# A four-stage attention and mixture-of-experts kernel: other queues and order for the first loads, a search by four experts, and another layout of the experts' weights

## The chip, the cores and the metric

The kernel runs on one core of a Trainium2 chip, as one launch. The metric is the device time of that core in microseconds (us); lower is better. A core has TensorE (PE; its weight loads are listed apart as PEld), VectorE (DVE), ScalarE (ACT), GpSimd (POOL) and SyncE (SP), which work side by side and wait for each other by semaphores. DMA transfers are issued by an instruction of SP, ACT or POOL and then run on 16 shared DMA engines.

## The reference

There are 8192 tokens (16 sequences of 512) with 256 features each, all in fp32. Four layers follow each other, each with a layernorm in front and a residual sum behind it:

```python
x = x + attention(layernorm(x))          # 16 heads of 16, rotary embedding, softmax
x = x + moe(layernorm(x))                # 64 experts
x = x + forget_attention(layernorm(x))   # linear attention with forget gates
x = x + moe(layernorm(x))                # the same weights as the second layer
```

The mixture of experts (`moe`) is the part that most of the change touches:

```python
probs = softmax(x @ router_w.T)                      # (T, 64)
topk_w, topk_ids = top_k(probs, 8); topk_w /= topk_w.sum(-1)
# each expert takes its first C = 128 tokens, in the order of the tokens
g, u = xb @ w_gate[e], xb @ w_up[e]                  # 256 -> 192
y = (silu(g) * u) @ w_down[e]                        # 192 -> 256
out = segment_sum(y * topk_w) + shared(x)            # shared: one expert for all tokens
```

The order of the 192 hidden features of an expert does not matter to the result, as long as gate, up and down agree on it.

## The kernel before, in words

`main` (L1453 to L1471) runs four stages one after the other. In the fast memory, data lies on 128 partitions.

**Stage 1, `attention` (L144 to L462).** The tokens are taken in 16 blocks of 512, and a block in 16 steps. Two tables, `dense` (L388) and `routed` (L403), say which piece of work stands at which step: `(queries, 1, 2)` at step 2 means chunk 2 of the projection of the block after this one. The loop runs them under `tc.manual_schedule`, which keeps the written order for the engines that it names (PE, DVE and ACT); for SP and POOL a scheduler puts the instructions in order. For each chunk of 128 tokens, `queries` projects (L229), copies (L237) and applies the rotary embedding with four operations on POOL (L242, L250 twice, L258) into a `pad`, which PE transposes (L283). Six pads are set to zero at the start (L179). The first loads are issued by SP: `wqkv_sb` (L168), `wo_sb` (L170), `rope_sb` (L172), x (L208), and ahead of them in the program the 32 small loads of `forget_bias` (L475), a bias of stage 3. mT, the row of maxima, is stored into the row qT by SP in each step group.

**`Part` (L1182 to L1426)** holds the router's and the shared expert's work for a routed stage: `moments`, `normed`, `features`, `logits` (L1313), `likely` (the softmax, L1325 to L1338), `choose` (top 8), `count`, `added` (running counts), `shared` (L1391) and `down` (L1413). In stage 1 it is woven into the attention's steps by the table `routed`. Its constructor loads the router's and the shared expert's weights by ACT's queue, and stores zeros behind the tokens (L1237). `Part.slots` (L1255) makes room for pairs of experts' weights; `Part.fetch` (L1266) loads a pair in three pieces by SP: gate, up and down, 384 KB each.

**Stage 2, `routed` (L873 to L1148).** The rest of the router's work for the last block comes first. The counts of tokens per expert and chunk of 128 tokens are stored and read back as `cw` (64 chunks on the partitions): L920 for all blocks but the last, L1130 for the last. `find` (L933 to L986) then searches the tokens of eight experts (`many = 8`): DVE compares `cw` (L942 to L947), PE picks the chunk's counts by matmuls (L954, L961), DVE counts and adds (L971 to L985), in two halves of four experts. `place` runs pieces of `find` between other work. The experts' loop has three steps in flight: `gather` (POOL, indirect load of 128 token rows, L998), `turned` (PE transposes, L1009), `widened` (gate and up, L1022: eight fp32 matmuls, each of two passes with a weight load of its own), `narrowed` (down, L1038, and an indirect scatter-add by POOL, L1049). The stationary operand of L1022 is the weights:

```python
lhsT=wm[:, e % 2, kd, ts(m % 2, FP)],     # FP = 96 of the FF = 192 columns, side by side
of = self.w_down[es].rearrange("e (k p) f -> p e k f", p=FP)
```

Pairs of weights ahead of the loop: 7 in stage 2, 4 in stage 4.

**Stage 3, `forget_attention` (L482 to L855)**, and **stage 4**, `routed` with `loads=True`: it loads x from stage 3's output (L914), does the router's work in 16 blocks, reads the counts back (L920), and runs the same experts' loop. `joined` (L1152) adds the two results and stores the output.

Of the kernel before, what the change touches and what calls it, by code (L numbers as in the profile page):

```python
# [9 lines left out]
F32 = mybir.dt.float32  # L10
# [27 lines left out]
class Block:  # L38


    def __init__(self, ctx: ExitStack, tc: tile.TileContext, T: int):
# [20 lines left out]
        self.stats = ctx.enter_context(tc.tile_pool(name="stats", bufs=2))  # L62
# [81 lines left out]
    def attention(self, x, x1, wqkv, wo, rope, part):  # L144
# [10 lines left out]
        with ExitStack() as c:  # L155
# [12 lines left out]
            nc.sync.dma_start(out=wqkv_sb, in_=wqkv.rearrange("(k p) f -> p k f", p=P))  # L168
            wo_sb = w.tile([P, KD, D], F32, name="wo_sb")
            nc.sync.dma_start(out=wo_sb, in_=wo.rearrange("(k p) f -> p k f", p=P))  # L170
            rope_sb = f1.tile([P, CB, 2 * HD], F32, name="rope_sb")
            nc.sync.dma_start(out=rope_sb, in_=rope.rearrange("(c p) f -> p c f", p=P))  # L172
# [4 lines left out]
            for i in range(CB + 2):  # L177
                pad = f1.tile([P, 2 * H, HP], F32, name=f"pad{i}")
                nc.gpsimd.memset(pad, 0.0)  # L179
                nc.gpsimd.memset(pad[:, H : 2 * H, HD : HD + 1], 1.0)  # L180
                pads.append(pad)
# [44 lines left out]
            def queries(b, i):  # L226
# [13 lines left out]
                t1 = f1.tile([P, 2 * H, HD], F32, name="t1")  # L240
                t2 = f1.tile([P, 2 * H, HD], F32, name="t2")
                nc.gpsimd.tensor_tensor(  # L242
# [5 lines left out]
                for half in range(2):  # L248
                    lo = half * (HD // 2)
                    nc.gpsimd.tensor_tensor(  # L250
                        t2[:, :, lo : lo + HD // 2],
                        qk2[:, :, :, 1 - half],
                        rope_sb[:, i, HD + lo : HD + lo + HD // 2]
                        .unsqueeze(1)
                        .to_broadcast([P, 2 * H, HD // 2]),
                        ALU.mult,
                    )
                nc.gpsimd.tensor_tensor(pads[b % 2][i][:, :, 0:HD], t1, t2, ALU.add)  # L258
# [104 lines left out]
            def output(b, i):  # L363
# [27 lines left out]
                3: [(queries, 1, 3)],  # L391
# [12 lines left out]
                0: [(part.added, -3), (part.likely, -2)],  # L404
                1: [(part.shared, -2, 0)],
                3: [(part.shared, -2, 1)],
# [6 lines left out]
                15: [(part.logits, -1)],  # L413
# [19 lines left out]
            with tc.manual_schedule(  # L433
                engines={nc.tensor.engine, nc.vector.engine, nc.scalar.engine}
            ):
                weights = (part.fetch(n, i) for n in range(3) for i in range(3))
                for s in range(-2 * steps, self.nblk * steps):
                    for count, n, work, *args in each(s):
                        if 0 <= n < count:
                            work(n, *args)  # L440
# [10 lines left out]
                part.likely(z - 1)  # L451
# [12 lines left out]
    def forget_bias(self, bqk):  # L464

        nc = self.nc
        sb = self.const.tile([P, 6], F32, name="bqk_sb")
# [11 lines left out]
        return sb  # L479
# [393 lines left out]
    def routed(self, part, loads=False):  # L873
# [7 lines left out]
        iota_c, down1, pairs = part.iota_c, part.down1, part.pairs  # L881
        with ExitStack() as c:

            def pool(n, **kw):
                return c.enter_context(
                    tc.tile_pool(name=f"f_{n}", bufs=n, side="left", **kw)
                )

            part.slots(pairs - len(part.slot), "left")
            w = c.enter_context(tc.tile_pool(name="f_w", bufs=1, side="left"))  # L890
# [3 lines left out]

            far = 4.0 * T
            first = w.tile([nch, 1], F32, name="first")
            nc.vector.tensor_scalar(first, self.iota_p[0:nch], float(P), far, ALU.mult, ALU.add)

            spare = w.tile([P, 1], F32, name="spare")
            nc.vector.tensor_scalar(spare, self.iota_p, far + T - P, None, ALU.add)  # L900
# [24 lines left out]
            many = 8  # L925
# [7 lines left out]
            def find(e0):  # L933
# [14 lines left out]
                yield  # L948
                cnt = self.small.tile([P, many], F32, name="cnt")
                place = self.small.tile([P, many], F32, name="place")  # L950
                for k0 in range(0, many, 4):
                    pn, ph = bank(), bank()
                    for k in range(k0, k0 + 4):
                        nc.tensor.matmul(  # L954
                            pn[:, ts(k - k0, P)],
                            lhsT=lies[:, k, :],
                            rhs=cw[:, e0 + k, :],
                            start=True,
                            stop=True,
                        )  # L960
                        nc.tensor.matmul(  # L961
                            ph[:, k - k0 : k - k0 + 1],
                            lhsT=lies[:, k, :],
                            rhs=first,
                            start=True,
                            stop=True,
                        )
                    yield
                    ks = slice(k0, k0 + 4)
                    near = p1.tile([P, 4, P], F32, name="near")  # L970
                    nc.vector.tensor_scalar(  # L971
                        near,
                        pn.rearrange("p (k t) -> p k t", t=P),
                        self.iota_p,
                        None,
                        ALU.is_le,
                    )
                    nc.vector.tensor_reduce(cnt[:, ks], near, AX.X, ALU.add)
                    nc.vector.scalar_tensor_tensor(
                        place[:, ks], ph[:, 0:4], -far, cnt[:, ks], ALU.add, ALU.add  # L980
                    )
                    yield
# [32 lines left out]
            def widened(e):  # L1015
# [3 lines left out]
                for m in range(4):  # L1019
                    wm = (wg, wu)[m // 2]  # L1020
                    for kd in range(KD):
                        nc.tensor.matmul(  # L1022
                            gu[:, m, :],
                            lhsT=wm[:, e % 2, kd, ts(m % 2, FP)],
# [36 lines left out]
            with tc.manual_schedule(  # L1061
# [4 lines left out]
                    nc.gpsimd.engine,  # L1066
                }
# [28 lines left out]
                if loads:  # L1096
                    for b in range(-4, nb + 1 + lag):
# [10 lines left out]
                        if nb - 4 <= b < nb:  # L1108
                            fetch(b - nb + 4)
                        if b == nb:  # L1110
                            chunks_before()
                            place(0, many)
                else:
                    z = nb - 1
                    for n in range(3, 5):
# [11 lines left out]
                    for i in range(CB):  # L1127
                        at = z * CB + i
                        queue = (nc.scalar, nc.sync)[i % 2]
                        queue.dma_start(out=cw[at : at + 1], in_=part.cum[:, ts(i, P)])  # L1130
                    part.shared(z, 1)
                    for n in range(5, pairs):
# [3 lines left out]
                    part.down(z, 0)  # L1136
                    place(0, many)
                    part.down(z, 2)
                ahead = 6
                for e in range(-ahead, E):  # L1140
                    run(e + ahead, E, gather)
                    place((e + 14) // many * many, 1)
# [39 lines left out]
class Part:  # L1182
# [6 lines left out]
    def __init__(self, ctx, k, x, y, weights, room, pairs, side):  # L1189
# [3 lines left out]
        nc, tc, T = k.nc, k.tc, k.T  # L1193
        self.pools = {
            n: ctx.enter_context(tc.tile_pool(name=f"r_{n}", bufs=n, side=side))
            for n in sorted({1, *room.values()})
        }
        w = self.pools[1]
        self.rows = k.dram.tile([T + P, ROW], F32, name="rows")
        self.counts = k.dram.tile([E, k.nch, P], F32, name="counts")  # L1200
        self.rw_sb = w.tile([P, KD, E], F32, name="rw_sb")
        nc.scalar.dma_start(out=self.rw_sb, in_=rw.rearrange("(k p) f -> p k f", p=P))

        self.wsg_sb = w.tile([P, KD, 2 * FF], F32, name="wsg_sb")
        for to, of, n in ((0, 0, FF), (FF, FF + P, FT), (2 * P, FF, P)):
            nc.scalar.dma_start(
                out=self.wsg_sb[:, :, to : to + n],
                in_=ws_gu[:, of : of + n].rearrange("(k p) f -> p k f", p=P),
            )
        self.wsd_sb = w.tile([P, 2, D], F32, name="wsd_sb")  # L1210
        nc.scalar.dma_start(out=self.wsd_sb[:, 0, :], in_=ws_down[0:P, :])
        nc.gpsimd.memset(self.wsd_sb[FT:P, 1, :], 0.0)
        nc.scalar.dma_start(out=self.wsd_sb[0:FT, 1, :], in_=ws_down[P:FF, :])

        self.hidden = []
        for i in range(room["hT"]):
            hT = w.tile([P, 2, BLK], F32, name=f"hT{i}")
            nc.gpsimd.memset(hT[FT:P, 1, :], 0.0)
            self.hidden.append(hT)
        self.iota_c = w.tile([k.nch, CAP], F32, name="iota_c")  # L1220
        nc.gpsimd.iota(
            self.iota_c,
            [[1, CAP]],
            base=0,
            channel_multiplier=0,
            allow_small_or_imprecise_dtypes=True,
        )

        self.down1 = w.tile([k.nch, k.nch], F32, name="down1")
        nc.gpsimd.memset(self.down1, 0.0)  # L1230
        nc.gpsimd.tensor_copy(self.down1[:, 1:], k.ident[0 : k.nch, 0 : k.nch - 1])

        with tc.tile_pool(name="r_z", bufs=1, side=side) as pz:
            zeros = pz.tile([P, ROW], F32, name="zeros")
            nc.gpsimd.memset(zeros, 0.0)
            for z in (self.rows, x, y):
                nc.scalar.dma_start(out=z[T : T + P, :], in_=zeros[:, 0 : z.shape[1]])  # L1237
# [14 lines left out]
        self.bank = None  # L1252

# [12 lines left out]
    def fetch(self, n, piece):  # L1266
# [6 lines left out]
        else:  # L1273
            to = both[0:FP, 2 * size :].rearrange("p (e k f) -> p e k f", e=2, k=2)
            of = self.w_down[es].rearrange("e (k p) f -> p e k f", p=FP)
# [154 lines left out]
def hybrid_block_kernel(  # L1430
# [29 lines left out]
    bqk_sb = k.forget_bias(b_bqk)  # L1460
    with ExitStack() as c:
        part = Part(c, k, attended, routed, moe, ROOM, 7, "right")
        k.attention(x, attended, a_wqkv, a_wo, rope, part)
# [79 lines left out]
```

## Time and profile before

| | us |
|---|---|
| median of 3 runs | 2860.42 (2859.69 to 2862.93) |
| profiled execution | 2867.78 |
| its span | 2865.9 |
| PE busy | 2595.7 |
| PEld busy | 1615.1 |
| DVE busy | 1870.4 |
| ACT busy | 1167.5 |
| POOL busy | 896.5 |
| TensorE clock granted, mean | 0.945 |

The page shows one execution, and everything read from it is compared with that execution's own 2867.78. Stage 1 ends near 1425 us, the experts' loop of stage 2 near 1720, stage 3 near 2270, the loop of stage 4 near 2790, and the rest is the final sum. Lines of a group read: engine, line, operation, output and inputs, shape, count. In the lines of the timeline the first number is the start, the second the time that the group takes, and the brackets hold the engine's idle time before it and what ended that.

### The profile page before, as it was taken

To read this page: it belongs to the slowest core of one execution; us is meant where nothing else is said; L and a number is where in the kernel's file an instruction comes from. 1 tells how busy PE (TensorE), PEld (TensorE's weight loads), DVE (VectorE), ACT (ScalarE), POOL (GpSimd) and SP (SyncE) were. 2 spreads that over 40 slices of the span, in tenths; PEclk is the share of its full clock that TensorE was granted. 3 is DMA by queue.
4 is the path that set the end of the run, shared out by engine and by line. 5 is a ranking of instruction groups with operands and counts; after the bars stand their busy time and mean duration, and the time that the engine had idled before them with its cause. 6 is when DMAs were issued, how large, how long until landed. Compare 5 with 4: busy or idle time off the path is not lost. (4 is left out here: it accounts for less than half of the span.)

```text
span 2865.9 us, 49079 instructions
## 1 busy us (share of the span) xinstructions
PE 2595.7 (91%) x18756; PEld 1615.1 (56%) x18756; DVE 1870.4 (65%) x4546; ACT 1167.5 (41%) x2291; POOL 896.5 (31%) x870
## 2 busy tenths in 40 slices
PE   4999999999999999999979986999999688879970
PEld 2444545544445544445459973666676565569860
DVE  2666666766666666666445636999999577845531
ACT  1565555655555655555512222334333212212220
POOL 4222221222221212220027775223322011127763
PEclk8899999999999999998979998999999879989995
DMA  1000111100111100001269973011110355339978
GB/s 60 1 6 21 33 34 35 32 20 20 34 33 34 33 20 27 27 25 35 68 164 255 257 168 105 25 48 54 48 38 20 96 164 134 99 100 255 253 176 344
DMA packets 210873, 243.75 MB, mean 85 GB/s; under 512 B 32847, under 2 KB 200911, under 8 KB 207567
## 3 DMA queue, kind: packets, MB, share of 16 engines
q1 hardware_dynamic: 181263, 192.22, 22.5%
q0 software_dynamic: 24576, 37.77, 6.7%
q10 hardware_dynamic: 4800, 10.62, 1.0%
q8 instruction: 150, 2.46, 0.4%
q14 instruction: 84, 0.69, 0.1%
HBM read 155.15 MB, written 84.74 MB: 84 GB/s over the span
## 5 line engine op out<-in xcount | busy, mean ns | idle before, releaser
L308 DVE TENSOR_REDUCE mx<-sc 128x1 f32<-128x512 f32 x1024 | 635.4, 682 | 418.0 <-PE sc L294 417.4
L334 ACT ACTIVATE pT<-sc 128x512 f32<-128x512 f32 x1024 | 528.7, 604 | 208.6 <-PE sc L294 206.8
L294 PE MATMUL sc<-kT,qT 16*128 16x512 f32 x2048 | 329.6, 607 | 1.7 <-DVE mx L308 1.7
L294 PE MATMUL sc<-qT,kT 17*128 17x512 f32 x2048 | 313.2, 647 | 0.0
L80 POOL TENSOR_SCALAR va<-mv 128x4 f32<-128x4 f32 x64 | 14.5, 226 | 765.2 <-DVE mv L74 540.1
L1022 PE MATMUL pb<-xeT,ws 128*96 128x128 f32 x2048 | 248.5, 275 | 0.2 <-DVE xeT L1011 0.2
L344 PE MATMUL sc<-pT,v 128*32 128x512 f32 x2048 | 239.6, 609 | 0.0
L1022 PEld LDWEIGHTS pb<-xeT,ws 128*96 128x96 f32 x2048 | 235.5, 166 | 0.6 <-DVE xeT L1011 0.4
L294 PEld LDWEIGHTS sc<-kT,qT 16*128 16x128 f32 x2048 | 159.5, 188 | 112.8 <-issue 62.3
L731 DVE SCALAR_TENSOR_TENSOR pT<-sc,of,left 128x256 f32<-128x256 f32 x512 | 205.8, 472 | 9.4 <-PE sc L714 9.3
L242 POOL TENSOR_TENSOR t<-qk,rope_sb 128x512 f32<-128x512 f32 x64 | 81.0, 1266 | 400.0 <-ACT qk L237 398.5
L868 ACT ACTIVATE th<-pb 96x256 f32<-96x256 f32 (+2 forms) x162 | 67.6, 425 | 304.1 <-PE pb L1022 216.0
L690 PE MATMUL pb<-feat,wqk_sb 128*128 128x512 f32 x384 | 176.3, 594 | 2.6 <-DVE left L673 2.6
L869 DVE SCALAR_TENSOR_TENSOR th<-th,pb 96x256 f32<-96x256 f32 (+2 forms) x162 | 76.4, 472 | 153.0 <-ACT th L868 102.6
L998 POOL DMA_INDIRECT xe<-rows,token x128 | 137.0, 1071 | 101.1 <-DVE token L985 62.7
L344 PEld LDWEIGHTS sc<-pT,v 128*32 128x32 f32 x2048 | 61.0, 112 | 170.5 <-issue 121.2
L294 PEld LDWEIGHTS sc<-qT,kT 17*128 17x128 f32 x2048 | 91.5, 185 | 93.9 <-issue 48.1
L1356 POOL TENSOR_TENSOR wt<-pr,chosen 128x256 f32<-128x256 f32 x32 | 23.2, 724 | 356.1 <-DVE chosen L1351 356.1
L229 PE MATMUL sc<-wqkv_sb,feat 128*128 128x512 f32 x256 | 129.5, 631 | 4.9 <-DMA wqkv_sb<-in_a_wqkv 4.9
L1038 PE MATMUL pb<-ws,he 96*128 96x256 f32 x512 | 131.9, 379 | 1.2 <-DVE he L870 1.2
L698 ACT ACTIVATE ez<-pb,bqk_sb 128x512 f32<-128x512 f32 x96 | 66.0, 687 | 134.3 <-PE pb L690 134.3
L72 DVE BATCH_NORM_STATS2 bn<-x 128x6 f32<-128x256 f32 x256 | 89.0, 408 | 41.6 <-POOL x L599 23.3
(175 smaller groups left out, 4557.0 us busy)
## 6 DMA issues: line engine op xcount, KB each, us to landing
ws<-in_w_gate SPq DMA_DIRECT2D x64, 384.0 KB
ws<-in_w_up SPq DMA_DIRECT2D x64, 384.0 KB
ws<-in_w_down SPq DMA_DIRECT2D x64, 384.0 KB
rows<-xn SPq DMA_DIRECT2D x32, 512.0 KB
routed<-y SPq DMA_DIRECT2D x32, 512.0 KB
x<-in_x SPq DMA_DIRECT2D x16, 512.0 KB
attended<-x SPq DMA_DIRECT2D x16, 512.0 KB
x<-attended SPq DMA_DIRECT2D x64, 128.0 KB
```

What stands on the lines that cost most here:

```text
L72: nc.vector.bn_stats(st[:, c, :], xt[:, c, :])
L229: nc.tensor.matmul(pq, lhsT=xnTs[b][:, kd, ts(i, P)], rhs=wqkv_sb[:, kd, 0 : 2 * D], start=(kd == 0), stop=(kd == KD - 1),)
L242: nc.gpsimd.tensor_tensor(t1, qk, rope_sb[:, i, 0:HD].unsqueeze(1).to_broadcast([P, 2 * H, HD]), ALU.mult,)
L294: nc.tensor.matmul(scs[j], lhsT=lhs[at : at + high, ts(i, P)], rhs=rhs[at : at + high, :], start=True, stop=True,)
L308: nc.vector.tensor_reduce(mxs[n][:, j, i : i + 1], sc, AX.X, ALU.max, negate=True)
L334: nc.scalar.activation(pT[:, j, :], sc, AF.Exp, scale=float(HD) ** -0.5)
L344: nc.tensor.matmul(pav[ts(j, HP), :], lhsT=vs[b % 2][:, i, 4 * hg + j, :], rhs=pT[:, j, :], start=(i == 0), stop=(i == CB - 1),)
L690: nc.tensor.matmul(pq, lhsT=wqk_sb[:, kd, ts(m, P)], rhs=xnTs[b][:, kd, :], start=(kd == 0), stop=(kd == KD - 1),)
L731: nc.vector.scalar_tensor_tensor(pTs[n][:, :, ts(s8, HD)], sc[:, :, ts(s8, HD)], of[:, s8 : s8 + 1], here, ALU.mult, ALU.mult,)
L998: nc.gpsimd.indirect_dma_start(out=xes[e], out_offset=None, in_=rows, in_offset=bass.IndirectOffsetOnAxis(ap=token[:, e : e + 1], axis=0),)
L1022: nc.tensor.matmul(gu[:, m, :], lhsT=wm[:, e % 2, kd, ts(m % 2, FP)], rhs=xeT[:, kd, :], start=(kd == 0), stop=(kd == KD - 1),)
L1038: nc.tensor.matmul(py[:, 0:D], lhsT=he[:, m, :], rhs=wd[:, e % 2, m, :], start=(m == 0), stop=(m == 1),)
```

## The change

- The constants of the search (`iota_c`, `down1`, `first`, `spare`) and the tile of zeros are made once for both routed stages, by DVE in part.
- First loads: wqkv, rope and wo go to ACT's queue, in this order. The memsets of the pads go from POOL to DVE. The rotary embedding of block 0's chunks 1 and 3 goes to DVE, with a later tile as its scratch.
- `forget_bias` becomes a generator; two of its loads are issued per step once the first block is under way. The loads of the router's and the shared expert's weights and the stores of zeros become `Part.begin`, issued by SP one step into the second pipeline block (stage 1), or at the head of stage 4.
- `likely` follows `logits` at step 15; `shared(-2, 1)` is put ahead of `queries(1, 3)` at step 3.
- SP is named in `manual_schedule` in stages 1, 2 and 4, so its DMAs keep the program's order.
- `find` searches four experts, in five pieces instead of seven. Stage 2's loop starts with one search of four instead of one of eight, and so does stage 4's.
- The last block's counts are read into `cw` by ACT's queue alone.
- 13 pairs of weights ahead in stage 2 (8 in one place, 5 more in the room that `Part` frees), 11 in stage 4.
- w_down is read so that a partition gets hidden features 2p and 2p + 1, in one piece of 2 KB instead of two of 1 KB; the columns of gate and up are then taken with a stride of 2.

The core of the diff:

```diff
@@ attention
-            nc.sync.dma_start(out=wqkv_sb, in_=wqkv.rearrange("(k p) f -> p k f", p=P))
+            nc.scalar.dma_start(out=wqkv_sb, in_=wqkv.rearrange("(k p) f -> p k f", p=P))
...
-                nc.gpsimd.memset(pad, 0.0)
+                nc.vector.memset(pad, 0.0)
...
+                if b == 0 and i % 2:
+                    eng, both = nc.vector, p2.tile([P, CB, D], F32, name="tok")
...
+                else:
+                    eng = nc.gpsimd
...
-                3: [(queries, 1, 3)],
+                3: [(part.shared, -2, 1), (queries, 1, 3)],
...
-                0: [(part.added, -3), (part.likely, -2)],
+                0: [(part.added, -3)],
...
-                15: [(part.logits, -1)],
+                15: [(part.logits, -1), (part.likely, -1)],
...
+                    nc.sync.engine,
...
+                    if s == 1 - steps:
+                        part.begin()
+                    if s >= 0:
+                        next(later, None)
@@ routed
-            many = 8
+            many = 4
...
-                            lhsT=wm[:, e % 2, kd, ts(m % 2, FP)],
+                            lhsT=wm[:, e % 2, kd, m % 2 : FF : 2],
...
-                        if nb - 4 <= b < nb:
-                            fetch(b - nb + 4)
+                        if nb - 5 <= b < nb:
+                            fetch(b - nb + 5)
                         if b == nb:
                             chunks_before()
-                            place(0, many)
+                            place(0, 5)
...
-                        queue = (nc.scalar, nc.sync)[i % 2]
-                        queue.dma_start(out=cw[at : at + 1], in_=part.cum[:, ts(i, P)])
+                        nc.scalar.dma_start(out=cw[at : at + 1], in_=part.cum[:, ts(i, P)])
...
                     place(0, 4)
-                    part.down(z, 0)
-                    place(0, many)
-                    part.down(z, 2)
+                    down(z)
+                    place(0, 1)
+                part.own.close()
+                n = len(part.slot)
+                part.slots(pairs - n, "left")
+                for n in range(n, pairs):
+                    fetch(n)
...
-                    place((e + 14) // many * many, 1)
+                    place((e + 10) // many * many, 2)
@@ Part.fetch
-            of = self.w_down[es].rearrange("e (k p) f -> p e k f", p=FP)
+            of = self.w_down[es].rearrange("e (p k) f -> p e k f", k=2)
@@ main
-        part = Part(c, k, attended, routed, moe, ROOM, 7, "right")
+        part = Part(c, k, attended, routed, moe, ROOM, 13, "left")
...
-        part = Part(c, k, forgot, routed, moe, ROOMY, 4, "right")
+        part = Part(c, k, forgot, routed, moe, ROOMY, 11, "left")
```

## The prediction

> **What bounds the kernel now.** I read the page's head first, then the time by engine in slices, TensorE's waits, and the stretches in which TensorE is idle.
>
> ```profile
> span 2865.9 us, 49079 instructions
> PE 2595.7 (91%) x18756; PEld 1615.1 (56%) x18756; DVE 1870.4 (65%) x4546; ACT 1167.5 (41%) x2291; POOL 896.5 (31%) x870
> PE   4999999999999999999979986999999688879970
> ```
>
> TensorE works 91% of the span; the low slices are the start, the passages between stages (slices 20, 24, 31 to 32, 35) and the final sum, which has no TensorE work. The waits name what ended each pause (total, times, longest):
>
> ```profile
> PE pb L586 <- DVE tok L98: 30.8, 1, 30.8
> PE sc L199 <- DVE tok L98: 21.7, 1, 21.7
> PE pb L1304 <- DVE xn L98: 20.4, 3, 18.4
> PE pb L930 <- DMA routed<-y: 13.2, 1, 13.2
> PE pb L930 <- DMA cw<-cum: 12.4, 1, 12.4
> PE sc L283 <- POOL pad L258: 10.7, 3, 3.7
> PE sc L229 <- DMA wqkv_sb<-in_a_wqkv: 4.9, 1, 4.9
> ```
>
> No wait names the experts' weights: they arrive ahead of their use already. Two windows (length, then busy time of PE, PEld, DVE, ACT, POOL; clock; DMA share; GB/s), one inside attention and one in the experts' loop, show that TensorE is the bound in both:
>
> ```profile
> 60.00:1280.00 1220.00, 1218.26 (x7897) 600.92 (x7898) 821.13 (x1800) 706.29 (x1387) 284.02 (x317) 0.99 0.08 26
> 1500.00:1560.00 60.00, 58.89 (x456) 55.55 (x455) 36.88 (x79) 15.35 (x36) 45.92 (x33) 1.00 0.98 250
> ```
>
> So the change can gain only in the passages, and lose wherever it makes TensorE's own stream longer. PE's instructions are as many before and after (10,469 in both orders). The profiled execution took 2867.8 us (span 2865.9 and 1.9 around it), 7.4 above the median of 2860.4. I sum differences and take them off the median.
>
> **1. Start.** Three lines of the timeline (start, length, idle before):
>
> ```profile
> 6.57 17.43 SPq L475 DMA_DIRECT2D bqk_sb<-in_b_bqk  x32
> 28.86 9.07 PE L229 MATMUL sc<-wqkv_sb,feat 128*128 128x512 f32 x16 [4.91 <-DMA wqkv_sb<-in_a_wqkv]
> 13.35 1.84 POOL L179 MEMSET pad<- 128x1024 f32 x2 [6.74 <-DMA routed<-zeros]
> ```
>
> SP issues 32 small bias loads for 17.4 us ahead of wqkv, so the first projection starts at 28.86. Besides, the pads' memsets hold POOL to 19, because they wait for the zeros' store, and the layernorm's power (L80, L82) stands behind them. After: wqkv leaves first on ACT's queue, the biases follow two per step, and the memsets are DVE's. x then sets the start. It landed at 6.0; sharing the transfer engines with wqkv's 0.79 MB, I put it at 7. From there by before's rows: statistics 1.8, POOL 1.3, DVE 0.6, first tok 0.4 and 0.5 of hand-over, transposes and copies 2.9, so the projection begins at about 14.5 to 15.5: 13.5 gained. The six memsets that DVE takes on (POOL took 0.95 each) are 4 to 6 us, done by about 7, beside the load of x; if x landed earlier they would be next to wait for.
> Then rope: POOL turns the four chunks in series, 1.27 + 1.43 + 1.27 = 4.0 each with a hand-over, so the pads are ready 20.7 after the projection's start (49.56 less 28.86). With every second chunk on DVE (0.68 + 2 x 0.42 + 0.68 = 2.2 by its rows of those sizes) POOL has two: 3.8 + 0.6 + 8.1 = 12.6. Gain 8. Begin's nine transfers (rw to zeros) go to SP behind the first two x, at about 0.45 each, 4 us, ahead of the first qT<-mT, which isn't ready for 20 us yet. Start together: 21.5; I take 21, and 15 to 23.
>
> **2. Attention.** Its PE order differs by the place of one part.shared call. `likely` moves 1 step earlier in DVE's order (L1325 to L1338 are 1.5 us of DVE a block); DVE is busy 821 of 1220, so I cost it at nothing. If that cover were gone it would be 16 blocks x 1.5 = 24. SP now keeps program order, so a store that waits holds the next qT<-mT and x; x is asked for two blocks (152 us) ahead. 0, bound 0 to +5.
>
> **3. Into the first experts.**
>
> ```profile
> 1445.18 8.98 SPq L1422 DMA_DIRECT2D routed<-y  x1
> 1451.77 1.17 ACTq L1130 DMA_DIRECT2D cw<-cum  x2
> 1457.20 1.23 SPq L1130 DMA_DIRECT2D cw<-cum  x2
> 1463.68 1.22 DVE L942 TENSOR_TENSOR lies<-cw,iota_c 64x1024 f32<-64x1024 f32 x1 [8.66 <-DMA cw<-cum]
> ```
>
> SP sits 9 us in the store of y, so half of cw's last pieces are issued 5.4 late. All four on ACT end at 1451.8 + 4 x 0.6 = 1454.1 instead of 1458.4: 4.3 gained (ACT's silu behind them is 1.2 later; its hT waits 15 us for use). Search: tokens of eight experts take 16.5 us (1463.7 to 1480.2), with down(z) between its halves. For four: three half-size compares (1.22 to about 0.65 each), 3.4 of matmuls, 2.0 of DVE, about 7.9: 8.6 earlier. The next four move into the loop, where each expert's search is 8 matmul passes of 0.11 less overlap, 0.73 us: +2.9. Net 10. But the extra pairs (5 x 1.18 MB, some 23 us at 250 GB/s) now travel beside the first gathers, which land 4 to 8 us after issue; I leave 2 for that. Taken 8, bounds 3 and 11.
>
> **4. The loops: pairs ahead and 2 KB pieces.** The window shows DMA at 0.98, yet PE idles 1.1 of 60 us, so I cost both at nothing; the cover is the weights' existing lead. Were it gone (gathers late), row "L1009 <- DMA xe" holds only 10.5 us in all.
>
> **5. The loops: gate and up read at stride 2.** This is the dangerous edit, since these loads are TensorE's:
>
> ```profile
> 1542.33 1.80 PEld L1022 LDWEIGHTS pb<-xeT,ws 128*96 128x96 f32 x16
> 1545.37 0.30 PEld L961 LDWEIGHTS pb<-first,lies 64*128 64x128 f32 x2
> 1545.59 0.30 PEld L954 LDWEIGHTS pb<-cw,lies 64*128 64x128 f32 x2
> 106.32 0.20 PEld L128 LDWEIGHTS sc<-ident,oT 128*128 128x128 f32 x2 [0.76 <-ACT pT L334]
> 1547.02 0.32 PEld L1009 LDWEIGHTS pb<-ident,xe 128*128 128x128 f32 x2
> ```
>
> Read the spacing, not the length. L1022's 16 loads follow each other every 0.11 us, which is what their matmuls take. L954 and L961, half of whose matmuls have one column, show what a plain load needs when nothing else limits it: 0.11 for 128 columns, so by proportion 0.083 for 96; a load has 0.026 of slack. L1009 is the only load here at stride 2 (xe as "(p k)"). Two of them last 0.32, one 0.195 to 0.22, so the second starts about 0.10 after the first; the same transposing load without stride (L128: two in 0.20, one 0.14) has 0.06. Stride 2 costs about 0.04 per 128 columns there, or a factor 1.7. [...] But a strided transposing load at 0.10 is still no slower than a plain unstrided one at 0.11. [...] If the 0.04 adds (0.03 for 96 columns): 0.113 against 0.11, at most +0.06 an expert. If it multiplies: 0.083 x 1.7 = 0.14, +0.03 x 16 = +0.48 an expert. With the search in the loop PE's period is 3.55 and POOL's 3.16 (gather 0.98, scatter 1.58, 0.3 after each), later PE 2.85 against POOL's 3.16: 55 x 0.48 and 9 x 0.17 are 28 a stage, 56 in both. I take +1, because the nearest row of its own, the spacing at L1009, stays under the matmul's pace; both ends stay.
>
> **6. The other passages.** Forget attention starts when the last scatter has landed; after, its weights load and its POOL copies need not stand beside it, but x and y still wait: -2 (-4 to 0). Second routed stage: first x<-forgot is issued at 2275.92 behind three weight loads (1.2 MB) and lands 7.3 later; now behind nine smaller ones: -2 (-5 to 0). Its end: TensorE waits 13.2 for y and counts, then hides the first gathers under 27 us of shared work; shared starts some 4 earlier, four experts' search moves into the loop (+2.9): -1 (-4 to +4). The final sum (324 GB/s) is untouched.
>
> **Sum.** -21 + 0 - 8 + 0 + 1 - 2 - 2 - 1 = -33: profiled 2834.8, median 2827.4; I say 2828. The granted clock can move it: TensorE is at half clock in several stretches of 5 to 50 us after pauses (clock 0.63 in 2260 to 2300, 0.66 in 1440 to 1500), and when each ends is not set by the kernel; +-14.
>
> **The rivals.**
> (a) Slower: the strided load is TensorE's bound in both expert loops, from the point where a load needs over 0.11 us. Price +56 against my +1, so 2828 + 55 = 2883. For it: TensorE is the bound there (58.9 of 60) and the L1009 spacing grew 1.7-fold. Against: that spacing stays below a plain load's. Chance 0.20.
> (b) Only part of the start comes: x lands late behind wqkv, or the memsets hold DVE's statistics, and first gathers are slowed by the prefetch. Gain 10 to 15, about 2848. For it: both x and wqkv then share the transfer engines. Against: before, x landed at 6.0 with wo and the shared weights in flight. Chance 0.13.
> (c) The gains are eaten: SP in program order holds qT<-mT or x in each attention block by 2 us, 32 in all, near 2860. Against: TensorE idles 1.7 of 1220 us with stores on the same queue. Chance 0.07, of which half ends within 0.2%.
> (d) The change doesn't do what it says: more pairs ahead and longer pieces bring nothing, as no wait names weights. That is in my sum already; start and search remain. A gain over 50 would need the loops to have waited for DMA after all. Chance 0.02.
> The main case has 0.58, and its own range is 2812 to 2844.
>
> **The numbers.** About 0.2% (5.7 us) is what a measurement of this kernel tells from no change. Faster: 0.58 + 0.13 + 0.02 = 0.73. Same: 0.04. Slower: 0.20 + 0.03 = 0.23. Range: from 2808 (main case with the lucky clock) to 2884, which takes in the middle of (a); about 0.12 lies above, 0.05 below.
>
> **What would show it.** Right: the first L229 matmul (of after, L254) near 15 and the first use of the last pad near 28; token of the first experts about 13 us sooner after attention's last sum; L1022's successor still 16 loads in 1.80 us, and the window in the loop at 3.5 us an expert. Wrong: 16 loads in 2.2 us or more; PE waits on wqkv or qT; a wait of L1009's transposes for xe over 20 us in all.

## The result, and the profile after

The changed kernel takes 2885.5 us (median of 4 runs, 2882.6 to 2888.4) against 2860.6 (2859.7 to 2862.9): 24.9 us slower, ratio 1.0086, 95% interval 1.0068 to 1.0103. The forecast was 2828. The time lies 1.5 us above the range, close to rival (a)'s 2883, but rival (a)'s mechanism is not the one that made it.

The head of the page of the changed kernel, its profiled execution (2888.4, span 2886.2):

```profile
span 2886.2 us, 49094 instructions
PE 2597.3 (90%) x18756; PEld 1638.5 (57%) x18756; DVE 1896.4 (66%) x4641; ACT 1168.1 (40%) x2291; POOL 879.0 (30%) x849
PE   7999999999999999999689959999999688599980
```

The first slice went from 4 to 7, so the start was gained. PE's busy time is the same within 2 us, but only in the sum: between attention's first and last score matmul it is 22 us less (1336.6 against 1358.7), in the two experts' loops 31 more (453.9 against 422.7). TensorE's waits in the changed kernel (line of the waiting instruction, what it waited for, total, times, longest):

```profile
PE pb L987 <- DVE lies L983: 42.7, 30, 4.0
PE pb L628 <- DVE tok L122: 30.1, 1, 30.1
PE pb L966 <- DMA cw<-counts: 24.9, 1, 24.9
PE pb L966 <- DMA cw<-cum: 17.8, 1, 17.8
PE sc L224 <- DVE tok L122: 13.5, 1, 13.5
PE pb L1042 <- DMA xe<-rows,token: 1.7, 2, 1.2
```

L987 is the search's matmul (L954 before). Before, it waited

```profile
PE pb L954 <- DVE lies L947: 8.5, 3, 3.3
```

and none of the three lay inside a loop. Of the 30 now, 4 lie ahead of the loops; the other 26, 13 in each loop, are 1.2 us each, 31 us together. L966 (L930 before) waits longer in both routed stages: 24.9 where it was 13.2, and 17.8 where it was 12.4.

The same moments in both traces (us from the span's start), read from the timelines, say where the difference arose:

| moment | before | after | after less before | gained or lost on the way |
|---|---|---|---|---|
| first score matmul | 55.5 | 37.2 | -18.3 | -18.3 |
| last score matmul of attention | 1416.0 | 1375.3 | -40.7 | -22.4 |
| stage 2: first gate/up matmul | 1492.0 | 1450.2 | -41.8 | -1.1 |
| stage 2: last down matmul | 1709.9 | 1696.0 | -13.9 | +27.9 |
| stage 4: first router matmul | 2289.8 | 2273.3 | -16.5 | -2.6 |
| stage 4: counts of earlier chunks (L930, L966) | 2525.0 | 2520.0 | -5.0 | +11.5 |
| stage 4: first gate/up matmul | 2562.4 | 2559.4 | -3.0 | +2.0 |
| stage 4: last down matmul | 2782.2 | 2803.4 | +21.2 | +24.2 |
| end | 2865.9 | 2886.2 | +20.3 | -0.9 |

(The spans differ by 20.3, the medians by 24.9: the profiled execution of before lies 7 us above its median, that of after 3.) Up to the first experts the change is 42 us ahead, 13 more than forecast. The two loops give back 52, and the end of stage 4's router work 11.5. That attention is shorter is not luck with the clock: between its first and last score matmul the granted clock stands at half speed for 58.0 us in both traces.

The loop's windows, two of the changed kernel (length, busy PE, PEld, DVE, ACT, POOL, clock, DMA share, GB/s), against 58.89 of 60 and a clock of 1.00 before:

```profile
1500.00:1560.00 60.00, 55.15 (x397) 51.81 (x395) 33.57 (x79) 13.68 (x32) 42.05 (x33) 0.94 0.90 230
1560.00:1620.00 60.00, 56.41 (x399) 53.57 (x398) 31.16 (x75) 12.83 (x30) 38.85 (x31) 0.91 0.77 188
```

TensorE stands still for 4 to 5 us of 60, and its granted clock falls below 1. Its weight loads take no longer than before. The same stretch of the trace:

```profile
1520.90 1.78 PEld L1055 LDWEIGHTS pb<-xeT,ws 128*96 128x96 f32 x16
```

Sixteen loads at stride 2 take 1.78 us, where sixteen without stride took 1.80; the run with plain loads, below, settles it. One search, in order of time:

```profile
1523.83 1.91 PE L1055 MATMUL pb<-xeT,ws 128*96 128x128 f32 x16
...
1525.57 1.03 PE L1071 MATMUL pb<-ws,he 96*128 96x256 f32 x4
1526.19 0.42 DVE L911 SCALAR_TENSOR_TENSOR th<-th,pb 96x256 f32<-96x256 f32 x1 [0.44 <-ACT th L910]
1526.64 0.42 DVE L912 SCALAR_TENSOR_TENSOR he<-th,pb 96x256 f32<-96x256 f32 x1
1526.98 0.68 DVE L983 TENSOR_TENSOR lies<-lies,begun 64x512 f32<-64x512 f32 x1
1527.80 0.46 PE L987 MATMUL pb<-cw,lies 64*128 64x128 f32 x2 [1.20 <-DVE lies L983]
1527.81 1.59 POOL L1082 DMA_INDIRECT routed<-ye,token  x1 [2.13 <-DVE lies L983]
```

Read it backwards. PE waits 1.20 us for `lies`. DVE makes `lies` 0.68 us long, but only behind the two silu pieces of the expert whose gate and up matmuls PE finished just before, and those come behind ACT's part. So PE waits out a round trip through ACT and DVE that normally lies beside its next matmuls. The cause is in the call `place(..., 2)`: it issues two pieces of the search at once, and the second pair is the product on DVE and the matmuls on PE that need it. Before, one piece was issued per expert, and the product was one expert old when PE came to it:

```profile
1534.99 1.21 DVE L947 TENSOR_TENSOR lies<-lies,begun 64x1024 f32<-64x1024 f32 x1
1537.39 0.49 PE L954 MATMUL pb<-cw,lies 64*128 64x128 f32 x2
```

In the changed kernel POOL's scatter also stands 2.13 us, and the trace names `lies` for it too, so the delay isn't made up on its side.

### The profile page after: what moved, and what is told of

The parts are those of the page before. It is cut to its first block, busy times and chain, and to the rows that moved or that the text cites. A ratio compares the mean times of both kernels' runs of the same rounds, so it can differ in the third digit from the quotient of the medians.

```text
span 2886.2 us, 49094 instructions
## 1 busy us (share of the span) xinstructions
PE 2597.3 (90%) x18756; PEld 1638.5 (57%) x18756; DVE 1896.4 (66%) x4641; ACT 1168.1 (40%) x2291; POOL 879.0 (30%) x849
## 5 line engine op out<-in xcount | busy, mean ns | idle before, releaser
L328 PE MATMUL sc<-kT,qT 16*128 16x512 f32 x2048 | 307.8, 607 | 1.4 <-DVE mx L342 1.4
L1055 PE MATMUL pb<-xeT,ws 128*96 128x128 f32 x2048 | 273.4, 292 | 1.6 <-DVE xeT L1044 1.4
L1055 PEld LDWEIGHTS pb<-xeT,ws 128*96 128x96 f32 x2048 | 258.4, 182 | 4.0 <-DVE xeT L1044 1.7
L1031 POOL DMA_INDIRECT xe<-rows,token x128 | 130.9, 1023 | 125.9 <-DVE token L1018 88.1
L1082 POOL DMA_INDIRECT routed<-ye,token x64 | 102.7, 1605 | 74.7 <-ACT ye L1079 47.0
```

The lines of the kernel that those rows point to most:

```text
L328: nc.tensor.matmul(scs[j], lhsT=lhs[at : at + high, ts(i, P)], rhs=rhs[at : at + high, :], start=True, stop=True,)
L1031: nc.gpsimd.indirect_dma_start(out=xes[e], out_offset=None, in_=rows, in_offset=bass.IndirectOffsetOnAxis(ap=token[:, e : e + 1], axis=0),)
L1055: nc.tensor.matmul(gu[:, m, :], lhsT=wm[:, e % 2, kd, m % 2 : FF : 2], rhs=xeT[:, kd, :], start=(kd == 0), stop=(kd == KD - 1),)
L1082: nc.gpsimd.indirect_dma_start(out=accs[e % 2], out_offset=bass.IndirectOffsetOnAxis(ap=token[:, e : e + 1], axis=0), in_=ye, in_offset=No ...
```

## The experiments

**The search's pieces one expert earlier.** PE's order stays; on DVE the compares and the product move ahead.

```diff
-                    place((e + 10) // many * many, 2)
+                    place((e + 11) // many * many, 3 if e == -ahead else (1, 2, 1, 1)[e % 4])
```

> The changed kernel, with the search's DVE pieces one expert earlier in the loop (two compares, then the product, then the matmuls, then the count, one expert apart), PE's order unchanged. Theory A (TensorE waits in each search for the product 'lies', which DVE does only behind the silu of the same expert: 30 waits, 42.7 us in all in the changed kernel, and the half-clock stretches that follow): the waits go and both loops run near 3.5 us an expert again, about 52 us less: 2833 us (2826 to 2846). Theory B (the weight loads at stride 2 bound TensorE in the loops): no change, 2885 us.

Measured: 2847.9 us (2842.8 to 2849.3), ratio to before 0.9951 (0.9934 to 0.9968), about 38 us less than the changed kernel. One window of its loop, later than the first experts:

```profile
1560.00:1620.00 60.00, 59.93 (x460) 56.20 (x459) 38.53 (x92) 15.33 (x36) 47.89 (x37) 1.00 0.81 194
```

PE is busy for 59.9 of 60 at full clock; the waits for `lies` are 11.1 us in 4 instead of 42.7 in 30, and the 4 are those ahead of the loops. Theory A holds and theory B falls. The time is 15 us above the forecast; the run with fewer pairs, below, finds about 20 us at the loops' starts.

**The plain weight loads and 1 KB pieces again.**

```diff
-                            lhsT=wm[:, e % 2, kd, m % 2 : FF : 2],
+                            lhsT=wm[:, e % 2, kd, ts(m % 2, FP)],
...
-            of = self.w_down[es].rearrange("e (p k) f -> p e k f", k=2)
+            of = self.w_down[es].rearrange("e (k p) f -> p e k f", p=FP)
```

> The changed kernel, with gate and up read side by side and w_down in pieces of 1 KB, as before. Theory A (the search's wait): no change, 2885 us within 6. Theory B (strided weight loads): the 50 us that the loops lost come back, about 2835 us.

Measured: 2883.9 us (2880.8 to 2886.8), ratio 1.0081 (1.0052 to 1.0109): the changed kernel's time. Rival (a) of the prediction falls.

**The search alone, in the kernel before.** Its edit is the change's `find`, with `many = 4`, `place(0, 5)`, `down(z)` between `place(0, 4)` and `place(0, 1)`, and `place((e + 10) // many * many, 2)` in the loop.

> The kernel before, with nothing but the search by four experts and its places in the loop as the changed kernel has them. Theory A: both loops lose about 25 us each to the wait for 'lies', and the first gathers come 4 to 9 us earlier in each: about +38, 2898 us (2885 to 2912), with some 40 us of waits for lies. Theory B (the loops' loss comes from the loads or the prefetch): only the earlier gathers count, about 2848 us.

Measured: 2901.9 us (2898.2 to 2905.6), ratio 1.0149 (1.0119 to 1.0179). Its largest wait of TensorE is the same as in the changed kernel, in number and size:

```profile
PE pb L951 <- DVE lies L947: 42.8, 30, 4.0
```

So the search is enough for nearly all of the loops' loss (50 of 52 us, see the table below), without strided loads, prefetch or SP's order.

**TensorE kept at work through the wait.** Six matmuls of the identity ahead of each search's matmuls in the loop; their result is overwritten.

```diff
                 pn, ph = bank(), bank()
+                for _ in range(6 if e0 else 0):
+                    nc.tensor.matmul(pn[:, 0:P], lhsT=self.ident, rhs=self.ident, start=True, stop=True)
```

> The changed kernel, with six more matmuls of the identity (about 1.3 us of TensorE work, the result is overwritten) ahead of each search's matmuls in the loop, so that TensorE works through the wait for 'lies' instead of standing still. Theory C (of the loss, half is the wait itself and half the half-clock stretches of 3.4 us that the pauses set off): the stretches go while the search's matmuls start no later, 20 to 30 us less, about 2860 us. Theory D (the wait alone): no gain, 2885 to 2890 us; if the wait were already shorter than the filler, up to 2895.

Measured: 2866.3 us (2852.8 to 2870.8 in 20 runs), ratio 1.0017 (1.0006 to 1.0028): about 20 us less than the changed kernel, with more work. The same two windows as above, in this run:

```profile
1500.00:1560.00 60.00, 58.06 (x456) 55.52 (x455) 33.15 (x79) 13.28 (x31) 43.86 (x34) 1.00 0.94 239
1560.00:1620.00 60.00, 59.96 (x470) 57.49 (x469) 33.70 (x80) 13.65 (x32) 45.14 (x34) 1.00 0.81 191
```

The clock is 1.00 again, and the search's matmuls still start only when `lies` is there. So theory C holds, and the loss has two parts. In the changed kernel the trace's clock records show nine stretches of 3.4 us at half clock in each loop, for 13 pauses; in this run the clock is 1.00 in both windows, and from 2600 to 2700 us too. In this kernel a pause of 1.2 us in about every 16 us was enough.

Of the loops' 52 us, TensorE's idle time makes 21: 31 more for `lies`, about 10 less for other things. Its busy time makes 31. Some 4 of these are the search of four experts that each loop has more (1.8 us by the trace); the other 27 fit the eighteen stretches at half clock. At half clock eight score matmuls took 2.09 us (at 52.13 in the changed kernel), at full clock 1.04 (at 67.08), so by estimate the stretches can cost 18 x 3.41 / 2 = 31 at most.

The loops' lengths (first gate/up to last down matmul, stage 2 and stage 4) put these runs side by side:

| kernel | stage 2 | stage 4 |
|---|---|---|
| before | 217.9 | 219.8 |
| after | 245.8 | 244.0 |
| e2_plain_loads | 246.0 | 246.0 |
| e3_search_in_before | 243.9 | 243.7 |
| e4_filler | 237.1 | 233.7 |
| e1_spread | 227.5 | 222.6 |
| e9_fewer_pairs (below) | 212.4 | 217.0 |

**Attention's tables put back**, both moves, and then `shared(-2, 1)` alone.

```diff
-                3: [(part.shared, -2, 1), (queries, 1, 3)],
+                3: [(queries, 1, 3)],
...
-                0: [(part.added, -3)],
+                0: [(part.added, -3), (part.likely, -2)],
...
+                3: [(part.shared, -2, 1)],
...
-                15: [(part.logits, -1), (part.likely, -1)],
+                15: [(part.logits, -1)],
...
```

> The changed kernel, with likely and shared(-2, 1) back at their old steps of attention. Theory E (these two moves take DVE's silu and softmax pieces out of the way of the maxima that TensorE's score matmuls wait for, 1.6 us a block in 13 to 14 blocks): about 22 us more, 2907 us (2900 to 2913), and attention's last scores come 22 us later against the first ones. Theory F (attention got shorter by SP's written order or by another thing): no change, 2885 us.

> The changed kernel, with shared(-2, 1) alone back behind queries(1, 3); likely stays with the logits. Theory E: one of the two places in a block is lost again, 0.7 to 0.9 us in 13 to 14 blocks, 10 to 13 us more: 2896 us. Theory F: 2885 us.

Measured: 2905.1 us (ratio 1.0165, 1.0147 to 1.0182) with both back, 2892.5 (1.0117, 1.0101 to 1.0134) with one. From the first to the last score matmul attention takes 1338.1 us in the changed kernel, 1348.5 with `shared` back and 1358.4 with both back (before: 1360.5). Each move is worth about 10 us of attention, and theory E holds. The timeline shows one of the two places. Before:

```profile
768.95 0.68 DVE L869 SCALAR_TENSOR_TENSOR th<-th,sc 64x512 f32<-64x512 f32 x1 [1.79 <-ACT th L868]
769.18 1.97 PE L294 MATMUL sc<-kT,qT 16*128 16x512 f32 x8
769.66 0.69 DVE L870 SCALAR_TENSOR_TENSOR hT<-th,sc 64x512 f32<-64x512 f32 x1
770.38 2.48 DVE L308 TENSOR_REDUCE mx<-sc 128x1 f32<-128x512 f32 x4
```

And after:

```profile
740.85 1.04 PE L328 MATMUL sc<-kT,qT 16*128 16x512 f32 x8
741.90 2.48 DVE L342 TENSOR_REDUCE mx<-sc 128x1 f32<-128x512 f32 x4 [1.60 <-PE sc L328]
```

In the first, the eight score matmuls span 1.97 us, because the maxima that free the score banks stand behind two silu pieces on DVE; in the second they span 1.04, both at a granted clock of 1.00. TensorE's busy time hides such a loss: the profile counts TensorE as busy for 1358.7 of attention's 1360.5 us before, and for 1336.6 of 1338.1 after.

**Biases later, in the kernel before.** `forget_bias` is called behind stage 2; nothing else.

> The kernel before, with the 32 loads of the bias issued after stage 2 instead of first; nothing else. Theory K (two things in series hold the start: wqkv's load behind the biases, and behind that the layernorm whose POOL step stands behind the pads' memsets): only the wait of 4.9 us for wqkv goes, since tok is still ready at 21; about 4 us less than before, 2855 us. Theory L (the biases alone hold the start): 14 us less or more, 2846 us.

Measured: 2849.9 us against 2856.2 of before on the same chip, ratio 0.9978 (0.9966 to 0.9990), 3 to 10 us less. The first score matmul comes at 49.4 instead of 55.5, the wait for wqkv is gone, and the wait for `tok` stays (21.7 before):

```profile
PE sc L199 <- DVE tok L98: 21.4, 1, 21.4
```

That is theory K: of the start's 18 us, the biases alone are 6. Next to this run, the changed kernel's projection begins another 8 us earlier, since its `tok` comes at 13.5, and 4 are gained between the projection and the scores, where half of rope is DVE's. No run moves the memsets alone, so that the 8 are theirs is read from the trace of before.

**Stage 4's weights fetched earlier**, on top of e1_spread.

```diff
-                        if nb - 5 <= b < nb:
-                            fetch(b - nb + 5)
+                        if nb - 10 <= b < nb - 5:
+                            fetch(b - nb + 10)
```

> e1_spread, and in stage 4 the five pairs of weights are fetched five blocks earlier, so that none stands on SP's queue between the last blocks' counts stores and the reads of them. Theory G (TensorE's wait of 24.9 us at the end of stage 4's router work, 13.2 before, comes from counts that travel behind 1.2 MB of weights, while SP stands in the read): the wait falls to 13 to 16 us, 8 to 11 us less than e1_spread: about 2838 us. Theory H (it comes from SP's written order alone, each read holding the next store): no change, 2848 us.

Measured: 2832.9 us (2831.1 to 2835.0), ratio 0.9912 (0.9895 to 0.9929), 15 less than e1_spread by the medians and 11 by the ratios, as before's own median was 2860.9 on e1_spread's chip and 2858.3 on this one. The wait fell from 24.1 us in e1_spread to this:

```profile
PE pb L966 <- DMA routed<-y: 13.1, 1, 13.1
```

That is before's 13.2. The changed kernel's SP queue shows what the edit removes:

```profile
2490.41 1.71 SPq L1405 DMA_DIRECT2D counts<-cum  x1
2499.52 0.27 SPq L956 DMA_DIRECT2D cw<-counts  x1
2499.89 0.37 SPq L1449 DMA_DIRECT2D routed<-y  x1
2500.31 0.49 SPq L1303 DMA_DIRECT2D ws<-in_w_gate  x1
...
2502.73 0.46 SPq L1405 DMA_DIRECT2D counts<-cum  x1
2512.80 0.27 SPq L956 DMA_DIRECT2D cw<-counts  x1
```

Each read of the counts is issued 7 to 10 us after the store before it: it waits for that store, and SP, in written order, holds the next store meanwhile. In this run, with the weights gone and the written order kept, the same reads follow 1.9 and 5.9 us after their stores, so theory H falls:

```profile
2468.64 0.51 SPq L1405 DMA_DIRECT2D counts<-cum  x1
2471.00 0.27 SPq L956 DMA_DIRECT2D cw<-counts  x1
...
2472.74 0.46 SPq L1405 DMA_DIRECT2D counts<-cum  x1
2479.12 0.27 SPq L956 DMA_DIRECT2D cw<-counts  x1
```

**Fewer pairs ahead**, on top of e8_fetch_early: `ROOM, 8` and `ROOMY, 5` instead of 13 and 11.

> e8_fetch_early with 8 and 5 pairs ahead instead of 13 and 11: nothing is fetched between the search and the experts' loop. Theory I (the extra pairs travel beside the first gathers and scatters, and the second group of eight experts runs at 4.2 us instead of 3.5): the loops' starts lose their waits for xe and scatters, 6 to 12 us less than e8_fetch_early: about 2829 us. Theory J (the long lead feeds the loops): weights come late, TensorE waits for ws, 2840 us or more.

Measured: 2811.5 us (2806.6 to 2813.4), ratio 0.9833 (0.9817 to 0.9850), 21 less than e8_fetch_early and twice what was expected. The extra pairs were fetched just as the loop began. POOL in e1_spread, with 13 pairs:

```profile
1480.83 0.99 POOL L1031 DMA_INDIRECT xe<-rows,token  x1 [0.31 <-issue]
1486.34 1.59 POOL L1082 DMA_INDIRECT attended<-ye,token  x1 [4.52 <-DMA attended<-ye,token]
```

A scatter waits 4.5 us for an earlier scatter of the same target to land. The second group of eight experts takes 4.2 to 4.4 us an expert there, 4.4 to 4.9 in e8_fetch_early and 3.4 here. TensorE's waits for gathered rows fell from 15.9 us in e8_fetch_early to 1.0. Theory J falls: no wait for weights appears with 8 and 5 pairs.

**Fewer pairs alone, in the changed kernel.**

> The changed kernel with 8 and 5 pairs ahead instead of 13 and 11; the search stays as it is. Theory O (in the changed kernel the waits for 'lies' bound the first groups of experts, so the scatters that wait for the extra pairs cost less than in e9): 3 to 10 us less, about 2878 us. Theory P (the pairs cost the same 21 us here): about 2864 us.

Measured: 2876.2 us, ratio 1.0071 (1.0046 to 1.0095). By the medians that is 9 us less than the changed kernel, by the ratios 4, and the intervals overlap (1.0068 to 1.0103), so a gain isn't shown; theory P's 2864 is outside. The two loops are 4 us shorter together. While the search holds the loop, the pairs cost little.

**The search of eight again**, in e9_fewer_pairs.

> e9_fewer_pairs with the search by eight experts of the kernel before, and its places. Theory M (well placed, the search by four is worth its earlier first gathers, 8.6 us in stage 2 and about 4 in stage 4, less 2.9 a stage in the loop): 6 to 10 us more than e9, about 2819 us. Theory N (the search by four brings nothing even then): equal to e9, 2811 us.

**Plain loads and 1 KB pieces**, in e9_fewer_pairs.

> e9_fewer_pairs with gate and up read side by side and w_down in pieces of 1 KB. Theory Q (neither the stride nor the pieces bear on the time, also where no search or prefetch stands in the way): 2811 us within 4. Theory B (the stride costs TensorE time): 5 us less or more. Theory R (the longer pieces relieve the transfer engines, which are at 0.9 there): 5 us more.

These two ran on one chip: 2822.5 us (ratio 0.9884, 0.9855 to 0.9913) with the search of eight, 2812.2 (0.9853, 0.9821 to 0.9885) with plain loads. Well placed, the search of four is worth about 10 us by these two medians, though their intervals overlap at the edges, and 15 by the ratio of e9_fewer_pairs (0.9833), whose interval lies apart. Theory M holds, if anything too low. The stride and the pieces are worth nothing that shows here either.

**The last counts.** `e13_two_queues` lets ACT and SP read in turn as before; `e14_weights_behind` keeps ACT alone and puts the fetch of pairs 6 and 7 behind the first search. Both on top of e9_fewer_pairs.

> e9_fewer_pairs with the last block's counts read by ACT and SP in turn, as before. In the changed kernel TensorE waits 17.8 us for these reads, 12.4 before. Theory S (four reads on one queue wait for each other's transfers; the second is issued 4.9 us after the first): the wait falls to 11 to 14, 4 to 6 us less than e9: 2806 us. Theory T (what delays them is the weights of two pairs that SP now issues meanwhile): also about 5 us less, since SP's own reads keep its weights behind. Theory U (neither; the counts of the other blocks land late): no change, 2811 us.

> e9_fewer_pairs with the two pairs of weights (6 and 7) fetched behind the first search instead of ahead of it; the counts stay on ACT's queue. Theory T (weights beside the reads): the wait falls by 4 to 6 us, 2806 us. Theory S (one queue by itself): no change, 2811 us. Both: half of it.

ACT's queue in e9_fewer_pairs, and then in e14_weights_behind:

```profile
1410.31 7.49 ACTq L1164 DMA_DIRECT2D cw<-cum  x4
1427.57 0.44 PE L966 MATMUL pb<-cw,down 64*64 64x64 f32 x2 [17.75 <-DMA cw<-cum]
```

```profile
1405.65 2.67 ACTq L1164 DMA_DIRECT2D cw<-cum  x4
1415.53 0.44 PE L966 MATMUL pb<-cw,down 64*64 64x64 f32 x2 [10.37 <-DMA cw<-cum]
```

Without the weights beside them, four reads on one queue are issued in 2.7 us instead of 7.5, and PE waits 10.4 us instead of 17.8. With two queues it waits 10.8. So the weights delay the reads, and theory S falls; in the trace of before, SP issued its own two reads at 1457.2 and the next weights at 1460.3, behind them. The whole time hardly follows: 2811.6 us for e14 (0.9826, 0.9810 to 0.9843) and 2808.7 for e13 (0.9816, 0.9797 to 0.9834), with intervals that overlap e9's. In e14's loop of stage 2, 216.8 us against 212.4, some of the 7 us are lost again; that its late pairs are the reason wasn't tried.

## Why the prediction was wrong, point by point

1. Start: right. The projection began at 15.5 (forecast 14.5 to 15.5) and 18.3 us were gained, against 21. The term that was too large is rope on two engines: the last pad came 14.9 us after the projection's start, not 12.6. DVE's share was sized by other rows of its own; beside POOL its two half products took 2.37 us and not 2 x 0.42, as the last section shows.

2. Attention, "I cost it at nothing": wrong by 22 us, in the kernel's favour. The step looked at whether DVE had time (821 of 1220 us), and not at what is queued on DVE in front of the maxima that free TensorE's score banks. E5 and e6 put 10 us to each of the two moves. (Two blocks are 170 us by the loads of x, 85 apart, and not 152; nothing hung on it.)

3. Into the first experts, -8: measured -1.1. The shorter search came for the most part: from L966 to the first gate/up matmul 21.9 us instead of 28.3, 6.4 of the 8.6 forecast. The counts did not: 4.3 us less was forecast, 5.4 more waiting was measured. The step counted issue times on ACT's queue and left out what SP would issue once it was free of its own reads.

The step that failed is in the same part: "The next four move into the loop [...] 0.73 us: +2.9". It priced the search by TensorE's work alone and put TensorE's wait for DVE's product at nothing; part 6 does the same with its "+2.9". `place(..., 2)` was in the diff, and the order of the pieces (product, then the matmuls that read it, in one call) was to be read there. The runs show 1.2 us of waiting at each of 13 searches in a loop, and the stretches at half clock that went with it: the two loops lost 52 us, and 50 with the search alone (e3).

The frame failed with it. "So the change can gain only in the passages, and lose wherever it makes TensorE's own stream longer": most of the loss came with hardly more work for TensorE, and 22 us were gained inside attention. None of the listed signs of being wrong showed (sixteen loads in 1.78 us, no wait for wqkv or qT, 1.7 us for xe); the list had no line for `lies`.

4. Pairs and pieces at nothing: the pieces are right (e2, e12). The pairs are right within some 10 us in the changed kernel (e11) and wrong for what the search would allow: once it no longer holds the loop, they cost about 20 us at the loops' starts (e8 against e9). I had left 2 us for this.

5. Strided loads, +1: right. The spacing at L1009 was the better guide than its length. No run shows the +1 itself: sixteen loads take 1.78 us at stride 2 and 1.80 without, and plain loads bring nothing in e2 (2883.9 us against 2885.5) or in e12 (2812.2 against 2811.5). Rival (a) named the right time for a wrong reason; its number must not be read as a hit.

6. The other passages, -5 in all: the way into stage 4 gained 2.6 in place of 4; its end lost 11.5 + 2.0 where -1 (-4 to +4) was forecast. The step left out that in this stage weights, stores and waiting reads share SP's queue: TensorE's wait grew from 13.2 to 24.9 us, and moving the weights alone brings it back to 13.1 (e8).

## What to carry to other kernels

When work is cut into pieces and issued between other work, look at the distance between a piece and its reader on another engine, not at the sum of the pieces: here one expert of distance hid the round trip (e1), and two pieces in one call laid it bare, 1.2 us at each of 26 searches. TensorE, busy for 1358.7 of attention's 1360.5 us, was still held by score banks that DVE freed late, about 20 us in all (e5), so a move on that other engine is priced by what it is queued in front of. Transfers issued early were not free either: five pairs moved brought TensorE's wait from 24.1 us to 13.1 (e8), and eleven pairs fewer were worth 21 us (e9). They belong where no small store, read or gather on the path travels beside them.

The fastest kernel of these runs, the changed one with the search spread, the fetches of stage 4 moved forward and 8 and 5 pairs, takes 2811.5 us, 1.7% less than the kernel before (0.9833, 0.9817 to 0.9850). With the last counts read by two queues it is 2808.7, which this measurement can't tell from it.

## What the runs showed of the hardware that had not been expected

TensorE, over 90% busy (55.15 and 56.41 of 60 us in the windows above), lost clock there (0.94 and 0.91): pauses of 1.2 us, once in about 16 us, went with stretches of 3.4 us at half clock, and useless matmuls in the pauses won about 20 us back (e4_filler).

The clock records also show which pauses were followed by a stretch. In the traces of before and of the changed kernel all changes of the clock lie on a grid with a step of 3.41 us. In the changed kernel's loops, 18 of the 26 pauses were followed by a stretch, from a grid point 1.7 to 2.8 us behind the pause, and 8 were not. The 8 began between 0.61 and 0.78 of a step behind a grid point, and the 18 between 0.82 of one step and 0.16 of the next. No run shifts the pauses against the grid or varies their length, so what decides between the two kinds is not shown.

In the rotary embedding, operations of DVE and POOL took longer beside each other. In the changed kernel's start operations of the two run side by side, and one of DVE's alone:

```profile
20.98 1.88 POOL L284 TENSOR_TENSOR t<-qk,rope_sb 128x256 f32<-128x256 f32 x2
22.18 2.37 DVE L284 TENSOR_TENSOR tok<-qk,rope_sb 128x256 f32<-128x256 f32 x2
24.58 1.64 DVE L292 TENSOR_TENSOR pad<-tok 128x512 f32<-128x512 f32 x1
29.68 0.69 DVE L292 TENSOR_TENSOR pad<-tok 128x512 f32<-128x512 f32 x1
```

DVE's sum takes 1.64 us beside POOL and 0.69 once POOL has finished; POOL's two products take 1.88, and took 1.43 in the kernel before, where DVE had none. DVE's two products at 22.18 have no row alone. No run takes the two engines apart, so what makes them slower stays open.
